# A three-scan state-space and attention kernel: three decay tiles, one PSUM bank each for other work and for state sums, eleven state buffers

## The chip, the cores and the metric

The kernel runs on one core of one Trainium2 chip, all in float32. The core has five engines with queues of their own, which wait for one another through semaphores: PE (TensorE, matrix products), DVE (VectorE), ACT (ScalarE), POOL (GpSimd) and SP (SyncE, which issues the DMAs here). PE writes only to PSUM, which has 8 banks of 512 float32 values in each of 128 partitions; ACT and DVE read and write PSUM and SBUF, POOL SBUF alone. The metric is device time in microseconds (us); lower is better.

## What is computed

Four layers on x of shape (2, 1024, 256). Layer 0 and layer 1 are selective state-space layers (one scan for layer 0; a forward and a reversed one for layer 1), layer 2 is linear attention, layer 3 softmax attention with 16 heads of 16. What the change touches is the scan:

```python
A = -jnp.exp(A_log)

def step(h, inp):
    dt_t, B_t, C_t, u_t = inp
    dA = jnp.exp(dt_t[:, :, None] * A)
    h = h * dA + (dt_t * u_t)[:, :, None] * B_t[:, None, :]
    y = jnp.einsum('bdn,bn->bd', h, C_t)
    return (h, y)
...
y = jnp.transpose(ys, (1, 0, 2)) + u * D_param
y = y * jax.nn.silu(z)
```

with 512 channels d, 16 states n, 1024 positions and two sequences. With two sequences and three scans a sequence there are six scans.

## The kernel before

**Tiles of a scan.** A tile is 128 partitions (32 channels by 4 states) by 1024 positions. A scan has 512 / 32 = 16 channel groups by 4 state groups = 64 tiles; six scans have 384. A tile takes these steps:

- `decay` (ACT): dA = exp(dt * A), from a spread of dt (`sp0`, dt of 32 channels copied to 128 partitions by a DMA) into a PSUM tile `dA` of two banks. `wide()` gives these tiles.
- `inputs` (POOL): the product of dt * u (spread `sp1`) with B (`bc0`) into an SBUF tile `hb`. This is the product with B.
- `tile` (DVE): the scan itself (`tensor_tensor_scan`, lines 959 and 963), then the product with C (line 966) into the `hb` tile. If the tile is "far", the scan writes into the `hb` tile and the product with C is issued on POOL instead (line 965).
- `fold` (PE): sums the states of 32 channels by a matrix product into a PSUM bank `ys` (line 990). `begin` starts each `ys` with u * D (line 976), and for the second scan of layer 1 with the y of the first (line 980). `finish` reads `ys` (ACT copy, or DVE product with the gate at line 998) and sends y to HBM.

**Order of the scan stage.** `chain` writes the order out by hand. It goes over 192 pairs (scan i, d, cp, k): each pair has two tiles of neighbouring channel groups with the same state group k (0 to 3). Four pairs make one `ys`. In each pair p, tiles 2p and 2p+1, `ahead(n, ...)` issues the decay or the input of a later tile n; other work is issued in two slots; the fold of pair p-1 comes at the end. A tile is made far by a running balance of counted DVE and POOL work (`lead`), at most one in a pair; its POOL product is issued behind the inputs of the second `ahead`. `load_spread` loads the spreads of the next group of tiles one group ahead, `load_rest` and `load_gate` the u, y and gate of it. Engines run their own queues: the order here is only that within each queue.

**Other work.** All of the layers that is no scan (norms, transposes, projections, residuals, layers 2 and 3 of the first sequence) is written as generators that the object `behind` steps through in the slots: a slot adds `rates[i]` columns of credit (2048 for the first two scans, 1250 to 1500 for the others), and a step costs the columns that it puts on PE, or at least 640. Slots also have limits for ACT and POOL work. `pipe` runs (make, use) pairs: make fills a bank with matrix products on PE, use empties it on ACT or DVE; as many fillings as there are banks (`banks["bank"]`) are made before the first is emptied. `projected` does the same for projections, and `ssm_inputs` makes dt and dt * u of a scan, with fillings `high(d, ch)` for the two halves of the positions, each read twice by ACT (`parts`). `residual` adds a filling to x on DVE (line 806).

**Memory.** The eight PSUM banks of the scan stage are two `dA` tiles (four banks), two `bank` for other work and two `ys`. In SBUF there are eight `hb` tiles, four `sp0` and three `sp1`.

**Attention.** After the scans the PSUM is divided anew (seven `sc`, one `av`); layer 3 of both sequences runs with layer 2 and 3 of the second as other work, with the `hb` tiles as exponentials.

Of the kernel before, what the change touches and what calls it, by code (L numbers as in the profile page):

```python
# [10 lines left out]
F32 = mybir.dt.float32  # L11
# [5 lines left out]
B, T, D, DI, N, R = 2, 1024, 256, 512, 16, 64  # L17
H, DH = 16, 16
P = 128
# [35 lines left out]
def kernel(ctx: ExitStack, tc: tile.TileContext, a: dict, out: bass.AP):  # L55
    nc = tc.nc
# [1 line left out]
    const = ctx.enter_context(tc.tile_pool(name="const", bufs=1))  # L58
    wp = ctx.enter_context(tc.tile_pool(name="wp", bufs=1))
    act = ctx.enter_context(tc.tile_pool(name="act", bufs=15))  # L60
    hbp = ctx.enter_context(tc.tile_pool(name="hbp", bufs=8))
    small = ctx.enter_context(tc.tile_pool(name="small", bufs=2))
    dram = ctx.enter_context(tc.tile_pool(name="dram", bufs=1, space=bass.MemoryType.DRAM))

# [5 lines left out]
    psum = []  # L70

    def wide():
        return psum[-1].tile([P, T], F32, tag="dA", name="dA_t", bufs=2)

    def bank(tag=None):
        tag = tag or mode["bank"]
        return psum[-1].tile([P, 512], F32, tag=tag, name=f"{tag}_t", bufs=banks[tag])

    banks = {"bank": 2, "ys": 2, "av": 1, "sc": 7}


    mode = {"bank": "bank", "scans": False, "tail": False, "least": 640}
# [486 lines left out]
    def ssm_inputs(key, u, w_xp, w_dt, dt_b, st):  # L569

        dbl = abuf((R + 2 * N, T))

        def low(ch):
            ps = bank()
            for k in range(4):
                mm(
                    ps[: R + 2 * N, :], w_xp[:, k, :], u[k][:, ts(ch, 512)],
                    start=(k == 0), stop=(k == 3),
                )
            return ps  # L580

        def take(ch, ps):
            act_copy(dbl[:, ts(ch, 512)], ps[: R + 2 * N, :])

        if key == "00":
            pss = [bank() for _ in range(2)]
            for k in range(4):
                for ch in range(2):
                    mm(
                        pss[ch][: R + 2 * N, :], w_xp[:, k, :], u[k][:, ts(ch, 512)],  # L590
                        start=(k == 0), stop=(k == 3),
                    )
            for ch in range(2):
                nc.vector.tensor_copy(dbl[:, ts(ch, 512)], pss[ch][: R + 2 * N, :])
        else:
            yield from pipe(*(
                (lambda ch=ch: low(ch), lambda ps, ch=ch: take(ch, ps)) for ch in range(2)
            ))
        st["bc"] = dbuf((2 * N, T), f"bc_{key}")
        save(2, st["bc"], dbl[R : R + 2 * N, :])  # L600
        if "first" in st:
            later(2, st["first"])


        st["dt"] = dbuf((2, DI, T), f"dt_{key}")

        def high(d, ch):
            held[0] += 1
            ps = bank()
            mm(ps, w_dt[:, ts(d, P)], dbl[:R, ts(ch, 512)], start=True, stop=True)  # L610
            return ps

        def parts(d, ch, ps, dt, dtu):
            held[0] -= 1
            act_f(dt[:, ts(ch, 512)], ps, AF.Abs, bias=col(dt_b, d))
            if key == "00" and d == 0:
                nc.vector.tensor_scalar(
                    dtu[:, ts(ch, 512)], ps, col(dt_b, d), 0.0, ALU.add, ALU.max
                )
            else:  # L620
                act_f(dtu[:, ts(ch, 512)], ps, AF.Relu, bias=col(dt_b, d))

        def both(d, o, x, y, op):

            if key == "00" and d == 0:
                nc.vector.tensor_tensor(o[:, :512], x[:, :512], y[:, :512], op)
                nc.gpsimd.tensor_tensor(o[:, 512:], x[:, 512:], y[:, 512:], op)
            else:
                far_op(o, x, y, op)

        two = banks["bank"] == 2
        pss = [high(0, ch) for ch in range(1 + two)]
        yield
        for d in range(4):
            dt, dtu = abuf(), abuf()
            parts(d, 0, pss[0], dt, dtu)
            if not two:
                pss.append(high(d, 1))
                yield
            parts(d, 1, pss[1], dt, dtu)  # L640
            yield
            act_f(dt, dt, AF.Exp, scale=-1.0)
            act_f(dt, dt, AF.Ln, bias=one)
            if d < 3:
                pss = [high(d + 1, ch) for ch in range(1 + two)]
            yield
            both(d, dt, dt, dtu, ALU.add)
            save(3, st["dt"][0, ts(d, P), :], dt)
            if key != "00":
                yield  # L650
            both(d, dtu, dt, u[d], ALU.mult)
            save(3, st["dt"][1, ts(d, P), :], dtu)
            later(3, lambda d=d: st["have"].append(d))
# [353 lines left out]
    def chain(scans, rates, early, mid, after):  # L1007

        pairs = [
            (i, d, cp, k)
            for i in range(len(scans)) for d in range(4) for cp in range(2) for k in range(NK)
        ]
        made = {"decay": {}, "inputs": {}}

        def ahead(n, kind):
            if n < 2 * len(pairs):
                i, d, cp, k = pairs[n // 2]
                made[kind][n] = getattr(scans[i], kind)(4 * d + 2 * cp + n % 2, k)  # L1020

        def fold(p):
            i, d, cp, k = pairs[p]
            if k == 0:
                scans[i].begin(d, cp)
            scans[i].fold(d, cp, k, [made["inputs"].pop(2 * p + j) for j in range(2)])

        def following(p):

            q = p - pairs[p][3] + NK  # L1030
            if q < len(pairs):
                i, d, cp, _ = pairs[q]
                return scans[i], 4 * d + 2 * cp

        s = scans[0]
        behind.until(lambda: s.st["have"])
        for c in range(2):
            for w in range(2):
                s.load_spread(c, w)
        s.load_bc(0, 1)  # L1040
        for k in range(1, NK):
            for w in range(2):
                s.load_bc(k, w)
        s.load_rest(0, 0)
        ahead(0, "decay")
        made["inputs"][0] = s.inputs(0, 0, nc.vector)
        ahead(1, "inputs")
        ahead(2, "inputs")
        mode["scans"] = True
        spent.update(ACT=0, POOL=0, DVE=0)  # L1050
        lead = 0
        for p, (i, d, cp, k) in enumerate(pairs):
            s = scans[i]
            nxt = following(p)
            final = d == 3 and cp == 1
            if d == 3 and cp == 0 and k == 0:
                early[i]()
            if final and k == 3:
                mid[i]()
            if k == 0 and nxt:  # L1060
                for w in range(2):
                    nxt[0].load_spread(nxt[1], w)
            if k == 1 and nxt:
                nxt[0].load_spread(nxt[1] + 1, 0)
            if final and i + 1 < len(scans):
                scans[i + 1].load_bc(k, 0)
            if k == 3 and nxt:
                nxt[0].load_rest(nxt[1] // 4, nxt[1] // 2 % 2)
            ahead(2 * p + 3, "inputs")
            ahead(2 * p + 1, "decay")  # L1070
            behind.slot(rates[i])

            ended = pairs[p - 3][:3] if p > 2 and k == 2 else None
            if ended and not scans[ended[0]].gate:
                scans[ended[0]].finish(*ended[1:])

            lead += 2 * (2200 + 1200 - 2300) + spent["DVE"] - behind.given["POOL"]
            spent["DVE"] = behind.given["POOL"] = 0
            far = lead >= LEAD
            if far:  # L1080
                lead -= 2300 + 1200
            lead = min(lead, 3 * 2300)
            rest = s.tile(
                4 * d + 2 * cp, k, made["decay"].pop(2 * p), made["inputs"][2 * p], far
            )
            if ended:
                if scans[ended[0]].gate:
                    scans[ended[0]].finish(*ended[1:])
                if ended[0] < i:
                    after[i - 1]()  # L1090
            if k == 3:
                s.load_gate(d, cp)
            ahead(2 * p + 2, "decay")
            ahead(2 * p + 4, "inputs")
            if rest:
                rest()
            if k == 1 and nxt:
                nxt[0].load_spread(nxt[1] + 1, 1)
            behind.slot(rates[i])
            s.tile(4 * d + 2 * cp + 1, k, made["decay"].pop(2 * p + 1), made["inputs"][2 * p + 1])  # L1100
            if final and i + 1 < len(scans):
                scans[i + 1].load_bc(k, 1)

            if p:
                fold(p - 1)
        fold(len(pairs) - 1)
        scans[-1].finish(3, 1)
        flush()
# [633 lines left out]
```

## Time and profile before

| | us |
|---|---|
| median of 3 runs | 2102.75 |
| lowest and highest run | 2097.81, 2104.69 |
| span of the profiled execution, first to last instruction | 2094.2 |

The profile is of one execution, whose own time the page gives as the span alone. Over the span (busy, share, instructions, mean granted clock of PE 0.851):

| engine | busy us | share | instructions |
|---|---|---|---|
| PE | 1592.7 | 76% | 8112 |
| DVE | 1748.3 | 83% | 1742 |
| ACT | 1140.8 | 54% | 1592 |
| POOL | 1365.8 | 65% | 666 |

The costliest groups of the scan stage (mean of one, busy, and the idle time of the engine just before them):

| operation | count | mean ns | busy us | idle before us |
|---|---|---|---|---|
| POOL input, L952 | 383 | 2436 | 918.7 | 62.9 |
| POOL product with C, L965 | 99 | 2387 | 236.3 | 16.3 |
| DVE scan into dA, L963 | 195 | 2286 | 445.8 | 43.8 |
| DVE scan into dA, L959 | 90 | 2285 | 205.7 | 11.8 |
| DVE product with C, L966 | 285 | 1224 | 349.0 | 22.1 |
| ACT decay, L133 | 384 | 1117 | 428.3 | 530.4 |
| PE fold, L990 | 1536 | 735 | 278.7 | 167.2 |

A line such as "POOL hb_t L952 <- PE ys_t L990: 28.7, 18, 4.0" in the list of waits says that POOL, ahead of an instruction of line 952 that writes an `hb` tile, waited 28.7 us in total, in 18 places, the longest of 4.0 us, until PE had done an instruction of line 990. "issue" stands where the profile shows nothing that was waited for. Other work fills tiles named bank_t. Line 133 is the helper of all ACT activations and line 95 that of most matrix products, so these are told apart by tile.

### The profile page before, as it was taken

What the parts mean: (1) busy time and instruction counts of PE and PEld (TensorE: products, weight loads), DVE (VectorE), ACT (ScalarE), POOL (GpSimd) and SP (SyncE); (2) the same over time, 40 slices, a digit from 0 to 9 for tenths busy, and PEclk for the clock granted to TensorE, in tenths of its full rate; (3) what the DMA queues carried; (4) which work ended last, traced back from release to release, by engine and by line L of the source; (5) the groups of instructions that cost most, each with busy time, mean ns of one, the idle gap of its engine ahead of it and who ended that gap; (6) DMA issues with size and microseconds to landing.
All of it is one profiled execution on the core that took longest, in us unless ns stands there. A gap on an engine that the chain in (4) does not pass through costs nothing. (4 is left out here: it accounts for less than half of the span.)

```text
span 2094.2 us, 22957 instructions
## 1 busy us (share of the span) xinstructions
PE 1592.7 (76%) x8112; PEld 605.6 (29%) x8112; DVE 1748.3 (83%) x1742; ACT 1140.8 (54%) x1592; POOL 1365.8 (65%) x666
## 2 busy tenths in 40 slices
PE   7576876389685637887955657834999999999997
PEld 3132213033141302222311333201544333333333
DVE  5798898898998999998998999998767657777763
ACT  4665775476546345664555455532154556656665
POOL 0799997998999999899998979997102111000000
PEclk9698988599797558988976978966899999999999
DMA  3673367264853555556763345343200111010001
GB/s 120 253 251 103 130 238 263 69 207 144 289 182 115 188 169 187 179 171 210 251 213 111 103 160 165 122 133 99 82 1 1 39 25 18 24 51 1 1 1 38
DMA packets 112503, 267.55 MB, mean 128 GB/s; under 512 B 16154, under 2 KB 40603, under 8 KB 112388
## 3 DMA queue, kind: packets, MB, share of 16 engines
q1 hardware_dynamic: 112388, 266.09, 38.2%
q8 instruction: 64, 1.05, 0.2%
q14 instruction: 51, 0.42, 0.1%
HBM read 195.91 MB, written 67.90 MB: 126 GB/s over the span
## 5 line engine op out<-in xcount | busy, mean ns | idle before, releaser
L952 POOL TENSOR_TENSOR hb_t<-sp,bc 128x1024 f32<-128x1024 f32 x383 | 918.7, 2436 | 62.9 <-PE ys_t L990 28.7
L133 ACT ACTIVATE dA_t<-sp,negA 128x1024 f32<-128x1024 f32 x384 | 428.3, 1117 | 530.4 <-DVE hb_t L966 446.4
L963 DVE TENSOR_TENSOR_SCAN dA_t<-dA_t,hb_t 128x1024 f32<-128x1024 f32 x195 | 445.8, 2286 | 43.8 <-ACT dA_t L133 29.0
L1442 DVE TENSOR_REDUCE mh<-sc_t 128x1 f32<-128x512 f32 x512 | 327.4, 684 | 114.2 <-PE sc_t L1433 110.6
L990 PE MATMUL ys_t<-hb_t,fold 128*32 128x512 f32 x1536 | 278.7, 735 | 167.2 <-POOL hb_t L965 110.5
L133 ACT ACTIVATE hb_t<-sc_t 128x512 f32<-128x512 f32 x512 | 276.7, 595 | 190.8 <-PE sc_t L1433 190.6
L966 DVE TENSOR_TENSOR hb_t<-dA_t,bc 128x1024 f32<-128x1024 f32 x285 | 349.0, 1224 | 22.1 <-DVE dA_t L959 0.5
L1433 PE MATMUL sc_t<-act_t 32*128 32x512 f32 x2048 | 337.3, 651 | 10.6 <-DVE mh L1442 8.8
L965 POOL TENSOR_TENSOR hb_t<-hb_t,bc 128x1024 f32<-128x1024 f32 x99 | 236.3, 2387 | 16.3 <-DVE hb_t L963 15.6
L799 POOL TENSOR_TENSOR act_t<-act_t,row 128x1024 f32<-128x1024 f32 x8 | 19.1, 2397 | 340.1 <-PE sc_t L99 191.9
L959 DVE TENSOR_TENSOR_SCAN dA_t<-dA_t,hb_t 128x1024 f32<-128x1024 f32 x90 | 205.7, 2285 | 11.8 <-POOL hb_t L952 7.4
L1473 PE MATMUL av_t<-hb_t,act_t 128*32 128x256 f32 x2048 | 164.7, 393 | 1.3 <-DVE act_t L1481 1.3
L95 PE MATMUL bank_t<-act_t,w_c_w 128*128 128x512 f32 x256 | 129.5, 656 | 37.0 <-ACT act_t L133 37.0
L133 ACT ACTIVATE act_t<-bank_t,cols 128x512 f32<-128x512 f32 (+1 forms) x206 | 129.6, 675 | 37.6 <-PE bank_t L95 29.5
L1433 PEld LDWEIGHTS sc_t<-act_t 32*128 32x128 f32 x2048 | 110.7, 186 | 121.4 <-issue 78.3
L990 PEld LDWEIGHTS ys_t<-hb_t,fold 128*32 128x32 f32 x1536 | 39.0, 119 | 362.7 <-POOL hb_t L965 149.5
L963 DVE TENSOR_TENSOR_SCAN hb_t<-dA_t,hb_t 128x1024 f32<-128x1024 f32 x61 | 139.0, 2278 | 4.3 <-ACT dA_t L133 3.9
L141 POOL TENSOR_TENSOR act_t<-act_t 128x1024 f32<-128x1024 f32 x50 | 119.2, 2384 | 0.2
L95 PE MATMUL bank_t<-act_t,w_dt_w 64*128 64x512 f32 x96 | 71.2, 876 | 43.9 <-ACT act_t L133 38.5
L99 PE MATMUL bank_t<-ident,act_t 128*128 128x128 f32 x128 | 34.3, 422 | 91.4 <-ACT act_t L133 91.2
L1473 PEld LDWEIGHTS av_t<-hb_t,act_t 128*32 128x32 f32 x2048 | 42.3, 108 | 191.5 <-issue 178.6
L1378 POOL MEMSET act_t<- 128x1024 f32 x8 | 7.6, 951 | 130.4 <-PE sc_t L1433 130.4
(178 smaller groups left out, 1811.6 us busy)
## 6 DMA issues: line engine op xcount, KB each, us to landing
sp<-dt SPq DMA_DIRECT2D x192, 512.0 KB, 5.5
bc<-bc SPq DMA_DIRECT2D x48, 512.0 KB, 6.8
dt<-act_t SPq DMA_DIRECT2D x48, 512.0 KB, 5.7
u<-act_t SPq DMA_DIRECT2D x24, 512.0 KB, 3.0
fu<-u SPq DMA_DIRECT2D x96, 128.0 KB, 3.4
y<-y SPq DMA_DIRECT2D x96, 128.0 KB, 3.6
g<-act_t SPq DMA_DIRECT2D x16, 512.0 KB, 5.4
fg<-g SPq DMA_DIRECT2D x64, 128.0 KB, 3.2
```

Source lines behind the costliest of these rows:

```text
L95: nc.tensor.matmul(o, w, x, **kw)
L133: nc.scalar.activation(o, x, func, **kw)
L141: nc.gpsimd.tensor_tensor(o, x, y, op)
L952: engine.tensor_tensor(e, self.sp[c, 1], self.bc[0][k], ALU.mult)
L959: nc.vector.tensor_tensor_scan(h[:, ::-1], dA[:, ::-1], e[:, ::-1], 0.0, ALU.mult, ALU.add)
L963: nc.vector.tensor_tensor_scan(h, dA, e, 0.0, ALU.mult, ALU.add)
L965: return lambda: nc.gpsimd.tensor_tensor(e, h, self.bc[1][k], ALU.mult)
L966: nc.vector.tensor_tensor(e, h, self.bc[1][k], ALU.mult)
L990: nc.tensor.matmul(self.ys[d, cp][at : at + DS, :], fold, e[:, ts(ch, 512)], start=False, stop=(k == NK - 1),)
L1433: nc.tensor.matmul(ps, w[r, ts(at, P)], x[r, ts(wide_at, 512)], start=True, stop=True)
L1442: nc.vector.tensor_reduce(mh[n][:, t, ch, j : j + 1], ps, AX.X, ALU.max)
L1473: nc.tensor.matmul(sums.av[32 * j : 32 * j + 32, ts(part, 256)], sts[b]["v"][t // 2][:, t % 2, 4 * g + j, :], es[j // 2][:, at : at + 256] ...
```

## The change

It does this:

- PSUM: three `dA` tiles (six banks) in place of two, one `bank` and one `ys` in place of two each.
- SBUF: eleven `hb` tiles in place of eight. The scratch that the program reserves for DMA descriptors (`dynamic_dma_scratch_size`) is set to 1024.
- Order: before the first pair the decays of tiles 0 and 1 and the inputs of tiles 0 to 4 are issued (before: decay 0, inputs 0 to 2). In pair p the decays of tiles 2p+2 and 2p+3 and the inputs of 2p+5 and 2p+6 are issued (before: decays 2p+1 and 2p+2, inputs 2p+3 and 2p+4).
- `finish` of a `ys` is issued in the second pair of the next group (k = 1) in place of the third, since the only `ys` bank is needed again at the end of that pair.
- The `sp1` spread of the next group's second channel group is loaded in the first half of the pair with k = 1, in place of the second half.
- `ssm_inputs` fills and empties one half at a time; before the scans start the second half uses the `ys` bank.

```diff
-    hbp = ctx.enter_context(tc.tile_pool(name="hbp", bufs=8))
+    hbp = ctx.enter_context(tc.tile_pool(name="hbp", bufs=11))
...
-        return psum[-1].tile([P, T], F32, tag="dA", name="dA_t", bufs=2)
+        return psum[-1].tile([P, T], F32, tag="dA", name="dA_t", bufs=3)
...
-    banks = {"bank": 2, "ys": 2, "av": 1, "sc": 7}
+    banks = {"bank": 1, "ys": 1, "av": 1, "sc": 7}
...
-            pss = [bank() for _ in range(2)]
+            pss = [bank(tag) for tag in ("bank", "ys")]
...
-            ps = bank()
+            ps = bank("ys" if ch and not mode["scans"] else None)
...
-        two = banks["bank"] == 2
-        pss = [high(0, ch) for ch in range(1 + two)]
+        ps = high(0, 0)
         yield
         for d in range(4):
             dt, dtu = abuf(), abuf()
-            parts(d, 0, pss[0], dt, dtu)
-            if not two:
-                pss.append(high(d, 1))
-                yield
-            parts(d, 1, pss[1], dt, dtu)
+            parts(d, 0, ps, dt, dtu)
+            ps = high(d, 1)
+            yield
+            parts(d, 1, ps, dt, dtu)
+            if d < 3:
+                ps = high(d + 1, 0)
             yield
             act_f(dt, dt, AF.Exp, scale=-1.0)
             act_f(dt, dt, AF.Ln, bias=one)
-            if d < 3:
-                pss = [high(d + 1, ch) for ch in range(1 + two)]
             yield
...
         ahead(0, "decay")
+        ahead(1, "decay")
         made["inputs"][0] = s.inputs(0, 0, nc.vector)
-        ahead(1, "inputs")
-        ahead(2, "inputs")
+        for n in range(1, 5):
+            ahead(n, "inputs")
...
-            ahead(2 * p + 3, "inputs")
-            ahead(2 * p + 1, "decay")
+            ahead(2 * p + 5, "inputs")
+            if k == 1 and nxt:
+                nxt[0].load_spread(nxt[1] + 1, 1)
+            ahead(2 * p + 2, "decay")
             behind.slot(rates[i])
 
-            ended = pairs[p - 3][:3] if p > 2 and k == 2 else None
+            ended = pairs[p - 2][:3] if p > 1 and k == 1 else None
...
-            ahead(2 * p + 2, "decay")
-            ahead(2 * p + 4, "inputs")
+            ahead(2 * p + 3, "decay")
+            ahead(2 * p + 6, "inputs")
             if rest:
                 rest()
-            if k == 1 and nxt:
-                nxt[0].load_spread(nxt[1] + 1, 1)
             behind.slot(rates[i])
...
-    nc = bacc.Bacc("TRN2", target_bir_lowering=False, num_devices=1)
+    nc = bacc.Bacc(
+        "TRN2", target_bir_lowering=False, num_devices=1, dynamic_dma_scratch_size=1024
+    )
```

## The prediction

> **What bounds the kernel now.** I read the busy time by stage first, then the chain of waits, then the waits inside the scan stage, then single stretches. A stretch of the windows view has its bounds and its length, then each engine's busy time with the count of its instructions:
>
> ```profile
> 63.00:1457.00 1394.00, 944.64 (x3304) 337.88 (x3304) 1285.33 (x883) 777.06 (x951) 1306.70 (x618) 0.80 0.51 173
> 1457.00:2094.00 637.00, 605.94 (x4704) 246.27 (x4704) 433.09 (x803) 334.97 (x605) 54.01 (x33) 0.96 0.10 27
> ```
>
> The columns are PE, weight loads, DVE, ACT, POOL, the granted clock, DMA. The 384 scans lie in the first stretch: of 1394 us POOL is idle 87 and DVE 109, so two engines bind together. The second, the attention, is PE's (606 of 637). The chain of waits ends the first stretch on POOL (start, length, what):
>
> ```profile
> 1410.15 9.44 POOL hb_t L952 x4
> 1419.60 2.31 POOL hb_t L965
> ```
>
> So the scan stage gets shorter only as POOL idles less, and longer as soon as anything holds up POOL or DVE. The waits of that stage (total us, times, longest):
>
> ```profile
> ACT dA_t L133 <- DVE hb_t L966: 446.4, 208, 13.2
> ...
> PE bank_t L95 <- ACT act_t L133: 116.3, 46, 12.7
> ...
> DVE dA_t L963 <- ACT dA_t L133: 29.0, 18, 5.1
> POOL hb_t L952 <- PE ys_t L990: 28.7, 18, 4.0
> ...
> POOL hb_t L952 <- DMA sp<-dt: 17.4, 4, 10.5
> ...
> POOL hb_t L965 <- DVE hb_t L963: 15.6, 4, 7.2
> ...
> POOL hb_t L952 <- issue: 14.1, 3, 7.0
> ```
>
> POOL waits for a free hb tile (28.7, and I count the 14.1 with it, below), for a scan that its far product needs (15.6) and for a spread (17.4). DVE waits 40.8 us for decays over all its scan lines (29.0 here). ACT's 446 us cost nothing by themselves: it is blocked because both decay tiles are full.
>
> **What the change may give.** *Third decay tile.* A decay starts one tile earlier; a tile takes DVE 2.29 + 1.22 = 3.51 us, so of the 40.8 us only the parts of single waits beyond that stay (5.1, 4.4 and 3.9: together 2.9). 38 us of DVE's waits can go, but the time follows only as far as POOL, with its 87 us of idle, follows. *Eleven hb tiles.* At most the 28.7 + 14.1 us go. But a far product, issued behind the pair's two inputs, now stands behind tile 2p+6 in place of 2p+4: two inputs later, 2 x 2.436 = 4.9 us; the fold of its pair waits for it (PE waits 110.5 us in 29 such places already), and so do the fillings queued behind that fold on PE. Two of the three new tiles go into that distance. I take half, 21 us. *Far waits.* The four waits (15.6, longest 7.2) get 4.9 us more cover: I take 12. Together **-33 us**; bounds 0 and -58 (28.7 + 14.1 + 15.6).
>
> **What it costs: one bank for other work.** Today PE may fill a bank while ACT empties the other. Afterwards each filling waits for the emptying before it, which stands in ACT's queue behind a decay, which waits for DVE; behind the waiting filling on PE stand the folds, and for these wait hb tiles and so POOL. A stretch shows PE saturated even with two banks, and POOL held up behind it:
>
> ```profile
> 468.33 1.07 PE L990 MATMUL ys_t<-hb_t,fold 128*32 128x512 f32 x8
> 473.14 8.83 PE L95 MATMUL bank_t<-act_t,w_c_w 128*128 128x512 f32 x16 [3.75 <-ACT act_t L133]
> 481.90 1.07 PE L976 MATMUL ys_t<-fu,dgD 64*64 64x512 f32 x4
> 482.91 1.06 PE L990 MATMUL ys_t<-hb_t,fold 128*32 128x512 f32 x8
> ```
>
> ```profile
> 484.12 4.78 POOL L952 TENSOR_TENSOR hb_t<-sp,bc 128x1024 f32<-128x1024 f32 x2 [5.81 <-issue]
> ```
>
> Two fillings run back to back (4.4 us each), the fold comes 14.6 us after the last, and POOL starts right after it: this is why I count "issue" as an hb wait. With one bank an emptying goes between the two. Its price: 684 ns on ACT, and the hand-over twice (a copy ended at 916.90, the weight load it freed began at 916.96): 0.8 us. From 100 to 1400 us other-work banks are read 260 times by ACT and 36 times by DVE: 296 x 0.8 = 237 us go into PE's stream, which idles 1300 - 901 = 399 us. On the mean it fits. In full stretches it doesn't; of those of 50 us, all tiles and then bank_t alone:
>
> ```profile
> 1300.00:1350.00 50.00, 46.88 (x170) 16.91 (x168) 48.84 (x29) 28.97 (x37) 50.00 (x22) 0.97 0.38 118
> ```
>
> ```profile
> 1300.00:1350.00 50.00, 34.87 (x82) 14.51 (x80) 0.00 (x0) 10.26 (x18) 0.97 0.38 118
> ```
>
> 46.9 + 18 x 0.8 = 61.3, an overrun of 11.3. So worked out, the stretches that overrun are those from 200 (2.2), 250 (1.7), 400 (0.4), 450 (3.3), 500 (5.2), 600 (0.4), 850 (1.4), 900 (5.8), 1000 (7.2), 1150 (4.0) and 1300 (11.3). Sum **+43 us**. Low bound 0: POOL's and DVE's lead over one another (up to some six tiles, 21 us) swallows each overrun and is regained between. High bound 86, twice it: inside a stretch the fillings come in bursts, and what a burst loses the calm part doesn't give back. I take the middle.
>
> *DVE as the reader.* The sixteen residual additions (L806) stand in DVE's own queue. A filling of out_w is 31.4 / 8 = 3.9 us; it now starts when the addition before it ends, plus 0.2 of hand-overs, plus 1.07 of a fold in every second slot: 4.1 to 5.2 us, against one tile of 3.51 us in between: DVE waits 0.6 to 1.7 us, where the fillings are one slot apart, as I take half to be: 8 x 1.1 = **+9 us** (0 to 16 x 1.7 = 27).
>
> *Head.* The four transposed fillings before the first scan alternate between two banks today; serially three emptyings more are exposed, 3 x (0.77 + 0.1) = **+3 us** (0 to 6). The first dt fillings keep two banks, since the second half uses the ys bank. The additional first decay (1.12 us) lies in ACT's wait of 2.9 us for the next spread, and the added inputs run on POOL.
>
> **Parts at nothing.** *One ys bank, finish a pair earlier:* the reading of ys stands on ACT or DVE ahead of the next begin on PE; its cover is the pair between (7.0 us of DVE); if that goes, PE waits for DVE's 0.67 us and its turn, once in four pairs. The new wait can be DVE's: the finish needs the last fold, which needs a far product two inputs later. POOL is then late by up to 4.9 us, but is itself busy, so nothing is lost where it binds (0; at most 48 x 1 us, a mean exposure of one hand-over and fold, 1.07). *The spread moved ahead of the slot:* the SP queue waits there for the same input product, which is itself issued a pair earlier; the y and dt writes behind it move with it. POOL still has two inputs between the freeing and the using, so its 17.4 us stay (0; -17 to +10). *Descriptor scratch:* every DMA of the page is issued by SP in hardware, none by POOL: 0. *Dt steps:* one more yield per d, one fewer per pipe; other work ends by 1400 us, the scans at 1457: 0. *Attention:* its seven sc banks and av are untouched, and ACT's waits there are for scores, not for hb: 0.
>
> **Sum:** -33 + 43 + 9 + 3 = +22 us. The profiled span of 2094.2 would be 2116. The span lies 8.6 us under the median of the runs (2102.75); I carry that difference: 2102.75 + 22 = **2125 us**.
>
> **A rule against the change.** After PE's idle 11.03 us at 1283.74 eight transposes took 2.81 us; seven us later the same eight took 1.10. The scan stage runs at a granted 0.80, the attention at 0.96. The Trainium skill ("TensorE: Matmul & The Clock Gate", section "A second HAM failure mode: psum-queue depth-cycling") says that cycling through PSUM banks leaves small idles between groups of matmuls, between which the clock swings and throughput falls. By the row only long idles cost, and the sum stays +22; by the rule every exposed emptying risks the slow clock, and the third rival would be the forecast.
>
> **Rivals.** *Decoupling wins.* If the slack of three decay tiles and three more hb tiles swallows the bursts, the 43 shrink to a third (14) and the whole 58 come in: -58 + 14 + 9 + 3 = -32, **2071 us**. For it: DVE's waits for decays are single events of at most 5.1 us. Against: counted in the trace, at the start of 155 of the 384 scans no more than that scan's own input was ready, so POOL binds there already and idles little. It decides where the overrun stays under 21 us, POOL's lead. *One wait for another.* The far distance eats the new hb tiles and the third decay covers just what the single bank adds: -33 + 33: **2103 us**. That the eleven tiles don't give more lead is in this case. *The clock drops.* If the stage falls from 0.80 to 0.65, the 587 us of other-work matmuls become 587 x 0.80 / 0.65 = 722; of the 135 more a third falls into full stretches, +45 on +22: **2170 us**. Against: exposed idles of 0.8 us are far below the 11.03 of the row.
>
> **Numbers.** Within 0.3% (6 us, about what these runs can tell from nothing) is "same". Forecast 0.47 (its own range 2109 to 2150), decoupling 0.33, one wait for another 0.10, clock 0.10. So faster 0.33, same 0.10, slower 0.57. The range goes down to 2066, leaving out a quarter of the decoupling case, and up to 2168, leaving out half of the clock case.
>
> **What would show it.** Right: PE's waits for ACT ahead of bank_t several times 46 in count; DVE's waits for decays gone in the calm stretches and back around 450 to 550, 1000 to 1050 and 1300 to 1350; POOL's waits for ys_t there too; L806's waits over 8.6 us; attention still 637 us. Wrong: POOL's idle under 40 us in the scan stage, or scans ending before 1440 us.

## The result and the profile after

| | before | after |
|---|---|---|
| median, us (lowest to highest) | 2103.72 (2097.81 to 2107.44) | 2238.77 (2235.48 to 2246.88) |
| runs | 4 | 4 |
| span of the profiled execution, us | 2094.2 | 2237.0 |
| last scan ends, us after the span's start | 1452.8 | 1595.6 |
| DVE idle in the scan stage, us | 109 | 236 |
| POOL idle in the scan stage, us | 87 | 229 |

The changed kernel takes 1.0657 times the time of before [1.063, 1.0683]: 135 us more, six times the 22 forecast. (The after column stands beside its own runs of before.) The windows of after by stage, columns as in the prediction:

```profile
68.00:1596.00 1528.00, 1016.99 (x3296) 348.93 (x3296) 1291.87 (x880) 778.10 (x953) 1298.86 (x619) 0.76 0.47 157
1600.00:2237.00 637.00, 607.35 (x4704) 247.43 (x4700) 433.78 (x803) 335.10 (x605) 54.08 (x33) 0.96 0.10 27
```

The attention is what it was, 637 us. The scan stage grew from 1394 to 1528 with the same work on DVE (1285 to 1292 us) and on POOL (1307 to 1299): everything lost is waiting. The waits of that stage in after (total us, times, longest):

```profile
ACT dA_t L133 <- DVE hb_t L964: 366.4, 154, 9.8
...
ACT act_t L133 <- PE bank_t L95: 187.9, 97, 6.2
...
PE bank_t L95 <- ACT act_t L133: 171.9, 97, 18.5
...
POOL hb_t L963 <- DVE hb_t L961: 83.7, 21, 16.3
...
POOL hb_t L950 <- PE ys_t L988: 53.4, 21, 5.8
DVE y L996 <- PE ys_t L988: 53.4, 13, 9.2
...
DVE act_t L804 <- PE bank_t L95: 39.4, 11, 11.9
...
DVE dA_t L961 <- ACT dA_t L133: 34.1, 12, 6.4
...
DVE qmx L1227 <- PE bank_t L95: 22.8, 4, 6.1
```

(Line 961 is the scan that was 963, 964 the product with C that was 966, 963 the far product, 950 the input, 996 the product of y with the gate, 804 the residual addition.) PE waits for ACT ahead of a filling in 97 places, where it was 46. New is the other direction: ACT, ahead of an emptying, waits for PE 187.9 us in 97 places; in before that was 27.9 us in 21. DVE, too, now waits for PE: for y (53.4, was 2.0), for the residual additions (39.4, was 8.5), for `qmx`, a reading by DVE inside layer 2 (22.8, was 0.5). Two of these lines as they were in before:

```profile
ACT act_t L133 <- PE bank_t L95: 27.9, 21, 3.5
...
DVE act_t L806 <- PE bank_t L95: 8.5, 4, 5.0
```

POOL's waits for hb tiles went up (28.7 to 53.4), those for scans from 15.6 to 83.7.

A stretch of the timeline of after shows how PE and ACT block one another (start, length, what; in brackets the idle time ahead of it and what ended it). PE:

```profile
473.59 1.98 PE L95 MATMUL bank_t<-act_t,w_xz_w 128*128 128x512 f32 x4 [0.78 <-ACT act_t L133]
...
479.27 1.98 PE L95 MATMUL bank_t<-act_t,w_xz_w 128*128 128x512 f32 x4
...
485.82 3.06 PE L95 MATMUL bank_t<-act_t,w_xz_w 128*128 128x512 f32 x4 [4.57 <-ACT act_t L133]
```

ACT in the same stretch:

```profile
472.85 0.69 ACT L133 ACTIVATE act_t<-bank_t,cols 128x512 f32<-128x512 f32 x1 [3.23 <-PE bank_t L95]
473.44 1.11 ACT L133 ACTIVATE dA_t<-sp,negA 128x1024 f32<-128x1024 f32 x1
...
480.38 1.28 ACT L133 ACT_TABLE_LOAD   x1
481.67 1.06 ACT L133 ACTIVATE act_t<-act_t 128x1024 f32<-128x1024 f32 x1
482.75 1.28 ACT L463 ACT_TABLE_LOAD   x1
484.04 1.12 ACT L133 ACTIVATE dA_t<-sp,negA 128x1024 f32<-128x1024 f32 x1
485.10 0.67 ACT L133 ACTIVATE act_t<-bank_t,cols 128x512 f32<-128x512 f32 x1
```

DVE:

```profile
485.26 2.30 DVE L961 TENSOR_TENSOR_SCAN dA_t<-dA_t,hb_t 128x1024 f32<-128x1024 f32 x1 [2.51 <-ACT dA_t L133]
```

At 472.85 ACT has stood 3.23 us ahead of an emptying until PE had filled the bank, and the decay of 473.44 stood behind it. The filling of 479.27 was done at 481.25; its emptying came at 485.10, behind other work, two loads of activation tables (1.28 us each) and a decay in ACT's queue, so PE stood 4.57 us and DVE 2.51. A hand-over with nothing else in the way is the first line, 0.78 us: that is about the 0.8 that the prediction multiplied.

Where the stage lost is uneven. By the starts of the six scans the lengths went from 237, 249, 231, 220, 239, 212 to 273, 270, 230, 213, 325, 217 us: the first (+36), the second (+21) and the fifth (+87) lost, the others not. The fifth scan of before and then of after, in the windows view:

```profile
1002.00:1241.00 239.00, 148.79 (x625) 64.74 (x624) 228.16 (x181) 119.67 (x154) 213.19 (x102) 0.79 0.49 163
```

```profile
1053.00:1379.00 326.00, 202.17 (x666) 84.13 (x663) 241.64 (x199) 131.28 (x172) 218.51 (x113) 0.65 0.38 124
```

DVE was busy 228 of 239 us there and is 242 of 326 now; PE, with seven per cent more matmuls, takes 36% longer over them at a granted clock of 0.65.

### The profile page after: what moved, and what is told of

Read it like the earlier page. It is cut to its first block, busy times and chain, and to the rows that moved or that the text cites. A ratio compares the mean times of both kernels' runs of the same rounds, so it can differ in the third digit from the quotient of the medians.

```text
span 2237.0 us, 22803 instructions
## 1 busy us (share of the span) xinstructions
PE 1666.7 (75%) x8112; PEld 617.5 (28%) x8112; DVE 1758.7 (79%) x1741; ACT 1141.8 (51%) x1592; POOL 1358.0 (61%) x667
## 4 chain that ended last, share of the span: by engine, by line
PE 42%; DVE 20%; POOL 15%; ACT 9%; issue 8%; DMA 4%; SPq 1%; DVEq 0%; ACTq 0%; POOLq 0%
PE bank_t L95 15%; PE sc_t L1432 12%; POOL hb_t L950 10%; DVE dA_t L961 6%; PE av_t L1472 6%; ACT act_t L133 4%; PE sc_t L95 4%; DVE dA_t L957 3%; POOL hb_t L963 3%; ACT dA_t L133 2%; PE ys_t L988 2%; DVE mh L1441 2%; DVE hb_t L964 2%; PE sc_t L99 2%; POOL act_t L141 1%
## 5 line engine op out<-in xcount | busy, mean ns | idle before, releaser
L950 POOL TENSOR_TENSOR hb_t<-sp,bc 128x1024 f32<-128x1024 f32 x383 | 905.3, 2389 | 102.0 <-PE ys_t L988 53.4
L961 DVE TENSOR_TENSOR_SCAN dA_t<-dA_t,hb_t 128x1024 f32<-128x1024 f32 x194 | 443.1, 2284 | 34.2 <-ACT dA_t L133 34.1
L988 PE MATMUL ys_t<-hb_t,fold 128*32 128x512 f32 x1536 | 288.3, 781 | 124.9 <-POOL hb_t L963 65.7
L963 POOL TENSOR_TENSOR hb_t<-hb_t,bc 128x1024 f32<-128x1024 f32 x100 | 236.1, 2361 | 85.2 <-DVE hb_t L961 83.7
L95 PE MATMUL bank_t<-act_t,w_dt_w 64*128 64x512 f32 x92 | 78.3, 944 | 87.7 <-ACT act_t L133 83.2
L95 PE MATMUL bank_t<-act_t,w_c_w 128*128 128x512 f32 x256 | 119.4, 609 | 17.4 <-ACT act_t L133 17.4
L974 PE MATMUL ys_t<-fu,dgD 64*64 64x512 f32 x192 | 74.3, 860 | 70.3 <-ACT y L137 33.1
L95 PE MATMUL bank_t<-act_t,w_xz_w 128*128 128x512 f32 x128 | 72.6, 695 | 30.4 <-ACT act_t L133 30.4
```

The costliest lines, as they stand in the source:

```text
L95: nc.tensor.matmul(o, w, x, **kw)
L950: engine.tensor_tensor(e, self.sp[c, 1], self.bc[0][k], ALU.mult)
L961: nc.vector.tensor_tensor_scan(h, dA, e, 0.0, ALU.mult, ALU.add)
L963: return lambda: nc.gpsimd.tensor_tensor(e, h, self.bc[1][k], ALU.mult)
L988: nc.tensor.matmul(self.ys[d, cp][at : at + DS, :], fold, e[:, ts(ch, 512)], start=False, stop=(k == NK - 1),)
```

## The experiments

Eleven kernels. Each was timed beside before on its own chip, whose median there lay between 2100.11 and 2102.66.

**One bank for other work, alone.** Before, with one `bank` and the dt steps that go with it; the two `ys`, eight hb tiles and two decay tiles stay.

```diff
-    banks = {"bank": 2, "ys": 2, "av": 1, "sc": 7}
+    banks = {"bank": 1, "ys": 2, "av": 1, "sc": 7}
...
-        pss = [high(0, ch) for ch in range(1 + two)]
+        ps = high(0, 0)
...
+            parts(d, 0, ps, dt, dtu)
+            ps = high(d, 1)
+            yield
+            parts(d, 1, ps, dt, dtu)
```

> The kernel before with one bank for other work in place of two, and the dt steps that go with it; everything else is as before (two decay tiles, two ys banks, eight hb tiles, inputs three and four tiles ahead). Theory 1 (the single other-work bank ties PE's fillings to the readers' queues, and this is the loss): most of the 135 us, so +90 to +140 us, with the fifth scan alone (87 us longer in the changed kernel) at least +50, and DVE's waits for bank_t over 50 us. Theory 2 (the single ys bank with the earlier finish is the loss): +10 to +40 us. Theory 3 (inputs and far products two tiles further apart are the loss): 0 to +40 us.

2244.40 us, 1.069 [1.0669, 1.0711], +143: the one bank by itself costs more than the whole change, and a little more than theory 1 gave it. Scan by scan it costs 46, 18, -3, 2, 71 and 5 us. Its waits on DVE, then on ACT, then on POOL (its lines are numbered as in after; `qmx` is 1226):

```profile
DVE dA_t L961 <- ACT dA_t L133: 69.7, 35, 7.4
DVE act_t L804 <- PE bank_t L95: 39.1, 11, 11.0
DVE hb_t L961 <- ACT dA_t L133: 35.6, 17, 5.6
DVE dA_t L957 <- ACT dA_t L133: 23.2, 13, 5.0
DVE qmx L1226 <- PE bank_t L95: 18.0, 4, 5.5
...
DVE hb_t L957 <- ACT dA_t L133: 3.0, 3, 1.3
```

```profile
ACT act_t L133 <- PE bank_t L95: 160.6, 90, 5.1
```

```profile
POOL hb_t L950 <- PE ys_t L988: 142.0, 45, 14.4
```

Waits for decays come to 69.7 + 35.6 + 23.2 + 3.0 = 131.5 us, where before had 40.8; DVE's waits for a bank to 72 with three smaller lines that are left out (7.7, 4.3 and 2.5), where before had 10. POOL's 142 us for hb tiles I read as the end of the same chain (DVE late, folds late, tiles late); the fourth experiment bears on it.

**One ys bank and the earlier finish, alone.**

```diff
-    banks = {"bank": 2, "ys": 2, "av": 1, "sc": 7}
+    banks = {"bank": 2, "ys": 1, "av": 1, "sc": 7}
...
-            ended = pairs[p - 3][:3] if p > 2 and k == 2 else None
+            ended = pairs[p - 2][:3] if p > 1 and k == 1 else None
```

> The kernel before with one ys bank in place of two and the finish one pair earlier, all else as before. Theory 1: within 10 us of before, because with two other-work banks PE's folds are done in time for the finish. Theory 2: +50 to +70 us (the changed kernel's DVE waits 55 us for ys at the finish, ACT 18 and PE 33 behind it). Theory 3: within 10 us.

2123.16 us, 1.0105 [1.009, 1.012], +22, between what the theories expected (within 10, and 50 to 70). DVE waits at the product of y with the gate for the gate's spread, which is still loaded when it was (19.9 us, 3 times), and for the last fold (18.9, 8 times). On PE the begin of the next `ys` waits:

```profile
PE ys_t L976 <- ACT y L137: 50.5, 8, 14.6
PE ys_t L976 <- DVE y L998: 39.1, 11, 8.3
```

**The gains, alone.** Eleven hb tiles, the small scratch, inputs five and six tiles ahead and the spread's place, with before's banks and decays; and beside it only the hb tiles and the scratch.

```diff
-    hbp = ctx.enter_context(tc.tile_pool(name="hbp", bufs=8))
+    hbp = ctx.enter_context(tc.tile_pool(name="hbp", bufs=11))
...
-            ahead(2 * p + 3, "inputs")
+            ahead(2 * p + 5, "inputs")
+            if k == 1 and nxt:
+                nxt[0].load_spread(nxt[1] + 1, 1)
...
-            ahead(2 * p + 4, "inputs")
+            ahead(2 * p + 6, "inputs")
```

> The kernel before with eleven hb tiles, the small descriptor scratch, inputs five and six tiles ahead and the spread loaded earlier; two decay tiles, two banks and two ys banks as before. Theory 1: -5 to -30 us, since hb waits of 43 us shrink. Theory 2: the same. Theory 3: +30 to +80 us, with POOL's waits for scans ahead of far products near the 84 us of the changed kernel (16 before).

> The kernel before with eleven hb tiles and the small descriptor scratch alone, the order of instructions unchanged. Theory 1 and theory 2: 0 to -20 us (hb waits shrink; a scratch of 1024 costs nothing, because no DMA is issued by POOL). Theory 3: the same, and clearly faster than the variant with inputs five and six ahead. If the small scratch itself costs time, slower than before by more than 5 us.

2073.73 us, 0.9871 [0.9843, 0.9898], -28; the tiles and the scratch alone 2085.69, 0.9912 [0.9886, 0.9939], -16. Both are faster than before, by 1.3 and 0.9 per cent, and theory 3 falls: inputs and far products further apart cost nothing by themselves. The first is the best version of this study, though the two intervals just overlap. Its waits on POOL:

```profile
POOL hb_t L965 <- DVE hb_t L963: 22.2, 8, 4.4
POOL hb_t L952 <- DMA sp<-dt: 19.8, 6, 11.0
...
POOL hb_t L952 <- PE ys_t L990: 7.1, 3, 3.5
```

The waits for hb tiles fell from 28.7 to 7.1; those for far products rose a little (15.6 to 22.2) instead of falling. Neither result shows a cost of the small scratch; no run has it alone.

**The gains with one bank.** The first experiment's edits and the deeper inputs together.

> The one-bank kernel with eleven hb tiles, the small scratch and inputs five and six tiles ahead; two ys banks, two decay tiles. In the one-bank kernel POOL waits 181 us for hb tiles (142 and 39), behind late folds. If this lateness of the folds is what makes one bank dear, the three tiles more pay here even more than the 28 us they pay with two banks: 30 to 80 us faster than the one-bank kernel (+65 to +115 on before). If POOL's waits for hb only follow from DVE, which waits for decays and for bank_t, the tiles pay nothing here: within 15 us of the one-bank kernel (+130 to +158).

2247.34 us, 1.0685 [1.0662, 1.0708], +145: against the one bank alone (+143) the deeper inputs give nothing. POOL's waits only change their place:

```profile
POOL hb_t L963 <- DVE hb_t L961: 99.8, 26, 16.6
POOL hb_t L950 <- PE ys_t L988: 35.7, 16, 5.6
```

142.0 for hb tiles became 35.7, and the 20.8 for scans became 99.8. Decays still cost DVE 76.2 + 37.2 + 22.6 + 1.8 = 138 us. So the lateness of POOL follows from the other engines' and does not make the bank dear. The count that the prediction made says the same: at the start of 8 of the 384 scans of this kernel no more than the scan's own input was ready (155 in before, 74 with the one bank alone), so POOL hardly sets the pace any more.

**The missing bank or the order?** Two banks stay, but other work is issued as if there were one: each filling is read before the next is made.

```diff
-            if len(waiting) == banks["bank"]:
+            if len(waiting) == 1:
                 last = waiting.pop(0)
...
-                if len(waiting) == banks["bank"]:
+                if len(waiting) == 1:
                     yield from ended(*waiting.pop(0))
```

> The order of instructions that one bank gives (one filling, then its reading, then the next filling; the dt steps likewise), but two physical banks for other work; all else as before. If the missing bank is the loss (PE may not fill while the reader is still queued), this is near before: -10 to +25 us. If the order of the steps is the loss (readings issued a step earlier, so that ACT and DVE stand in front of a filling that isn't done), near the one-bank kernel: +100 to +143 us.

2127.30 us, 1.0109 [1.0082, 1.0136], +25. This kernel issues the same steps as the one-bank kernel and differs from it in the bank alone, so of the 143 us about 25 go with the order of steps and 118 with the bank that isn't there. ACT's waits for fillings in this kernel:

```profile
ACT act_t L133 <- PE bank_t L95: 47.3, 29, 3.8
```

Against 160.6 with one bank: a free second bank lets PE fill ahead of the reading even when the order of issue is strict.

**A second bank for DVE's readings alone.** The first experiment, with a bank of its own (`rd`) for every second filling that DVE reads.

```diff
-    banks = {"bank": 1, "ys": 2, "av": 1, "sc": 7}
+    banks = {"bank": 1, "ys": 2, "rd": 1, "av": 1, "sc": 7}
...
+    def second(i):
+        return "rd" if i % 2 and not mode["tail"] else None
```

> One bank for what ACT reads, as in the one-bank kernel, but a second one, and two fillings ahead, for what DVE reads in its own queue (residuals, masked k, the maxima of q, the inner and outer products of layer 2). In the one-bank kernel DVE waits some 70 us for bank_t (9 before) and 128 us for decays (41 before). If these are two separate losses, this is 45 to 75 us faster than the one-bank kernel (+70 to +100 us on before), and nearly all of the gain lies in the fifth scan. If DVE's waits for bank_t are only where one common lateness shows, it moves on to the decays and the gain is under 20 us.

2216.83 us, 1.0534 [1.0506, 1.0563], +114: 29 us (of 143) come back, between the two expectations. The fifth scan, which holds such readings, is 257 us long instead of the first experiment's 309, but others are longer (the first 292, was 284; the last 234, was 218). DVE's waits for the residual additions' banks fell from 39.1 to 17.4 us, and those for decays rose from 131.5 to 148. This kernel has two banks for other work, like the one with the order of one (+25), but ACT's readings have only one of them, and most of the loss stays.

**The changed kernel with two decay tiles**, the decays issued as before:

```diff
-        return psum[-1].tile([P, T], F32, tag="dA", name="dA_t", bufs=3)
+        return psum[-1].tile([P, T], F32, tag="dA", name="dA_t", bufs=2)
...
-            ahead(2 * p + 2, "decay")
+            ahead(2 * p + 1, "decay")
...
-            ahead(2 * p + 3, "decay")
+            ahead(2 * p + 2, "decay")
```

> The changed kernel with two decay tiles, and decays one and two tiles ahead as before; one bank, one ys bank, eleven hb tiles and the rest as changed. By the sum of the single edits (one bank +143, one ys bank +22, eleven hb tiles and inputs further ahead -28) it is +137 us, so the third decay tile is worth about nothing (within 10 us of the changed kernel). If the third decay tile pays its 38 us of DVE waits, this is +165 to +180 us.

2256.99 us, 1.0722 [1.0694, 1.075], +154: the third decay tile is worth 18 to 19 us in the changed kernel, again between the two expectations. Without it DVE waits 56.3 + 21.7 + 16.2 + 5.6 = 100 us for decays; with it 34.1 + 9.0 + 7.0 + 4.7 = 55, and 53.4 instead of 27.5 for y: a part of what it saves is waited for elsewhere.

**The changed kernel with the finish half a pair later**, behind the pair's second tile:

```diff
-            if ended:
-                if scans[ended[0]].gate:
-                    scans[ended[0]].finish(*ended[1:])
...
             s.tile(4 * d + 2 * cp + 1, k, made["decay"].pop(2 * p + 1), made["inputs"][2 * p + 1])
+            if ended:
+                if scans[ended[0]].gate:
+                    scans[ended[0]].finish(*ended[1:])
```

> The changed kernel with the gated finish on DVE issued behind the second tile of its pair in place of the first. In the changed kernel DVE waits 55 us for ys and 14 to 20 for the gate at the finish. If this place costs for itself, 30 to 60 us faster than the changed kernel (+75 to +105 on before). If the waits at the finish only show that PE is late with its folds behind the fillings, the wait goes elsewhere (decays, far products, hb) and it is within 15 us of the changed kernel.

2233.10 us, 1.0622 [1.0589, 1.0655], +131. The waits ahead of y fell from 53.4 to 16.2, and the time only by 4 to 6 us: the intervals of this run and of the changed kernel overlap. Decays took the place (59.0 + 16.7 + 10.8 + 4.2 = 91, from 55). So removing most of the largest single line among DVE's waits bought next to nothing.

**One filling a slot.** In a slot other work stops after the first step that has put matmuls on PE (`work[0]` counts their columns). First with one bank, then, as the control, with two banks and the deeper inputs.

```diff
+                at = work[0]
                 cost = self.step()
...
+                if work[0] > at:
+                    break
```

> The one-bank kernel with at most one PE-issuing step of other work in a slot, so that two fillings never stand in one slot with their readings between them; later work is forced where a scan needs it. If the loss of one bank (+143 us) comes mainly from fillings and readings that alternate inside a slot, while the decay stands behind them on ACT, this is +30 to +90 us on before. If each filling costs its time wherever it stands (PE waits for a reading that waits for a decay that waits for DVE), it stays within 20 us of the one-bank kernel: +120 to +165 us, more if the other work comes late and is forced.

> The control with two banks: the variant with eleven hb tiles and inputs five and six tiles ahead (-28 us on before), and the same limit of one PE-issuing step in a slot. If the limit itself is neutral with two banks, within 10 us of that variant (-40 to -18 us on before). If bursts hold PE up with two banks too, faster than that variant by over 10 us; if the other work comes late and is forced, slower than before.

With one bank 2220.20 us, 1.0569 [1.0546, 1.0592], +120; the control 2138.18, 1.0174 [1.0155, 1.0193], +38, where the same kernel without the limit has -28. By the recorded expectations the first lies at the low end of "each filling costs its time wherever it stands", and the second is the case of work that comes late and is forced. The limit costs about 66 us with two banks, probably since work that is put off is forced through in a burst later: in the control POOL waits 47 us in two places for ACT and DVE 88 us in twelve for decays. With one bank it gains 23 in spite of that. Under the limit the two kernels are 82 us apart, and 28 of these are the deeper inputs, which are only in the control: some 54 us for the one bank instead of 143. That would make fillings and readings taking turns inside one slot a good part of the 143. But the limit changes more than that, and with one bank the deeper inputs were worth nothing, so the two experiments don't settle it.

## Why the prediction was wrong

The sign was right; the time lies 71 us above the range's top of 2168. Built up in one order, each step as the difference of two kernels that were both timed against before, the 135 us divide so: one bank +143; the deeper inputs on top of it +2 (145 - 143); one `ys` and the earlier finish on top of these +10 (154.5 - 144.7); the third decay tile -19 (135.1 - 154.5).

**"One bank for other work", "+43 us ... Low bound 0 ... High bound 86": this step failed.** With the reader DVE (+9) and the head (+3) the prediction had 55 us for what the first experiment measured as 143. It went wrong in three places.

*The price was the best hand-over.* 0.8 us was an emptying that starts at once. Behind a filling in the one-bank kernel ACT's first reading started 0.98 us after its end on average (213 cases, 26 of them over 3 us; median 0.04), so a turn takes 0.98 + 0.68 + 0.05 = 1.7 us: most are quick, and a few long ones make half of the sum. Put into the prediction's own list of stretches, 1.7 would give some 225 us of overrun, more than the 143, so the price was not the only fault. The prediction itself had said that the emptying "stands in ACT's queue behind a decay, which waits for DVE", and then charged nothing for that.

*Only one direction was charged.* The prediction counted PE's waits for ACT, as work that no longer fits into PE's stream. With one bank ACT also waits for PE, 160.6 us ahead of emptyings, and the decays behind these in ACT's queue are late: DVE's waits for decays went from 40.8 to 131.5 us, +91, the largest piece of what DVE lost. With two banks in the order of one the two fall together, to 47.3 and 51 us. It took ACT's 446 us of waiting for free decay tiles as slack. It is slack only while no emptying that has to wait stands ahead of the decay; the order of the queue decides, not the sum of idle time.

*An average over 50 us hides what happens in a slot.* Overruns were sought in stretches where PE's work exceeded 50 us. The first scan lost 36 us with PE busy 186 of 273, and the fifth 87 with PE busy 202 of 325; no 50 us in these two scans hold more than 42 us of PE's work. The prediction's list gave the first scan 4 us of overrun, the fifth 11 and the sixth 11; with the one bank alone they lost 46, 71 and 5. The number of turns doesn't tell it either: with the one bank the fourth scan has 52 readings by ACT and lost 2 us, the first has 67 and lost 46. Why these scans and not others is not shown; 26 of DVE's 36 readings lie in the fifth, and 32 of the stage's 42 loads of activation tables in the first two.

**"DVE as the reader", +9 (0 to 27): too small.** Only the sixteen residual additions were counted. Waits of DVE for a bank grew from 10 to 72 us, and `qmx` and its like were left out of the sum; a second bank for these readings gave 29 us back.

**"Parts at nothing: One ys bank, finish a pair earlier", 0 (at most 48): +22 alone, +10 in company.** Its range held. The cover named, the pair between finish and begin, wasn't enough (PE's begin waits 50.5 + 39.1 us), and the gate's spread, not moved along, was the thing late next; that one the prediction didn't name.

**The gains, -33 (0 to -58): right in size where their condition holds, in part by luck.** With two banks the deeper inputs gave 28. But hb waits fell by 21.6 + 9.2 us (the second are the "issue" waits, 14.1 to 4.9) against the 21 taken, while the 12 from far waits didn't come (they rose by 7 on the line shown): two errors that offset one another. The third decay tile, which had no term of its own in the sum, gave 18 to 19, with one bank. But behind one bank the deeper inputs gave nothing (+2, within the intervals): POOL's lead didn't shorten a stage in which DVE waits for ACT and PE. Gains and costs were added as if they were independent; there the sum itself is wrong.

**Attention and head: right; scratch: no cost seen.** The attention's span is the same, the scans start 3.1 us later (67.62 against 64.53, predicted 3).

**What would show it.** PE's waits ahead of bank_t in number (97, from 46) and the residual's waits over 8.6 (39.4) came as foretold; "decay waits gone in the calm stretches" did not show in the total (55 us, where it was 41), and POOL's waits moved to far products.

**The rivals.** Decoupling (2071) is refuted as a forecast, yet 2071 is, by chance, nearly what the deeper inputs reach with two banks (2074, with 28 us of gain and not 58): its lead is real, the bank taken for it costs more. "One wait for another" fell too. The clock: the granted mean of the stage went from 0.80 to 0.76, and in the fifth scan from 0.79 to 0.65. PE's time on other work grew from 601 to 654 us. So the stage's 0.65 of this rival was reached in the fifth scan alone. In the one-bank kernel the stage has 0.77, and PE is idle a third of it. PE's busy time in the stage is 1009 us there and 945 in before, for the same work. As every queue's order is fixed, slower matmuls can delay the end by no more than they take longer, so the clock's own share is at most some 65 of the 143 us (an estimate); how much of these a full clock would give back no run here separates, and this stays open. Not tried either: three decay tiles with two banks each for other work and sums, which would take ten PSUM banks where there are eight (nine with one for sums).

## What to carry to other kernels

A single buffer between two engines with queues of fixed order cost both here: price it by what stands ahead of the reader in its queue and behind it, not by the reader's own duration, and look at both engines' waits. Before taking a buffer away to pay for another, run each half alone: here the deeper inputs alone gain 28 us, and the bank alone loses 143. A gain that works through lead on one engine was worth nothing once other engines set the pace, so don't add gains and losses that share a path.

## What the runs showed of the hardware

In the scan stage I counted PE's idle gaps (over 20 ns) ahead of matmuls into bank or ys tiles that began at the full clock, and whether the granted clock was half 1 us after PE's next start:

| idle | before: gaps, share at half clock | after: gaps, share |
|---|---|---|
| under 1 us | 29, 0.03 | 67, 0.04 |
| 1 to 2 us | 24, 0.08 | 22, 0.14 |
| 2 to 3.5 us | 24, 0.54 | 24, 0.50 |
| 3.5 to 6 us | 14, 1.00 | 20, 0.95 |
| over 6 us | 13, 1.00 | 4, 1.00 |

The stretch shown above has both ends: after 0.78 us of idle four matmuls took 1.98 us, after 4.57 us the same four took 3.06. The Trainium skill ("TensorE: Matmul & The Clock Gate", section "HAM oscillation — how this bites in real kernels") gives as its rule that PE should have no idle gaps above about 3.4 us. The runs agree: above that length nearly every gap cost the full clock; but from 2 to 3.5 us half of them did. The rule weighed in the prediction, of small idles between groups of matmuls, is not borne out for gaps under 1 us: their number more than doubled, and 3 to 4 per cent of them ended the full clock.

With all listed DMAs issued by SP, the descriptor scratch of 1024 and three more tiles were together worth 16 us; a cost of the scratch, if it has one, is smaller than what the tiles give. No run has eleven tiles without it.
